# Attention with software-pipelined steps: a unit's first values half a step later, reciprocals of 64 columns, and the maxima's rows by six transfers

## The chip, the cores and the metric

The kernel runs on one core of one Trainium2 chip. The metric is the device time of one execution in microseconds (us), and lower is better. The median of three runs of the kernel before is 2694.99 us (2693.69 to 2695.18).

## The reference

Two sequences of 2048 tokens with 512 features go through one decoder layer with 16 heads of 32 features. All is in float32.

```python
x = x + attn(layernorm(x))      # Q, K, V = projections; scores = Q K^T / sqrt(32), rotary angles on Q and K
                                # softmax over all 2048 keys, times V, then W_o
x = x + xattn(layernorm(x))     # h = x ctx^T, gelu (tanh form), times ctx (77 rows)
x = x + ffn(layernorm(x))       # x sign(W)^T * scale + bias, clipped to +-100
```

## The kernel before

The work goes sequence by sequence (B = 2). `project_batch` makes Q, K and V for 16 chunks of 128 tokens. `Attention.run` then does the attention. It is this function that the change touches.

**Units and steps.** A unit is 256 queries (HQ) of one group g of four heads; there are NU = 32 units per sequence. A unit has STEPS = 8 steps of 256 keys each (two chunks c of 128). A step has two halves in `run`: the first does the scores of heads 0 and 1, the second those of heads 2 and 3. So a unit has 16 halves, and the document speaks of "step 1, second half" and so on.

**A half on TensorE.** The scores of two heads (`scores`, L603) go into banks `st`, while the maxima of the other two heads (`maxima`, L484) run on the other 32-row groups of the array. The maxima are those of a later unit, AHEAD = 11 steps in front. Each maxima matmul fills a bank of the pool `ps_s`, which has three. VectorE reduces it (L496) and so frees the bank. ScalarE takes the exponentials (L744), and POOL adds the two chunks of keys (L746). Then TensorE does the values of the step before (`weigh`, L621: four matmuls of 256 columns, chunk 0 in the first half by `first_half`, chunk 1 in the second by `second_half`) and the totals of the step before that (`total`, L635: four matmuls of 128 columns). A unit's totals begin two steps after the unit itself, so step 1 has none. At the end of step 0's second half the totals of the unit before are closed.

**The scores carry their maximum.** `st` isn't written anew in each step: the unit begins by writing minus the maximum of each query into it (`lower`, L584, a matmul of a row of ones with `mrow`), and each step adds the product of Q with a difference of keys (`key_steps`, `wrap_around`). The maximum is split into three bfloat16 parts (`split_maxima`, step 4), so `mrow` has three rows for each head, at partitions 32h, 32h + 1 and 32h + 2, in two column halves c.

**The rows' way.** In step 5's second half, `turn_maxima` transposes the parts on VectorE (L526), writes the square to DRAM (L528) and reads it back into `mrow` by small transfers (L532), all from SyncE's queue. The next unit's `lower` needs them.

**The division.** `divide` is a generator: ScalarE copies numerators and totals out of the accumulator bank (L649, the pool `ps_acc` has one), VectorE takes reciprocals (L655), POOL multiplies into the q tile (L658). `finish` takes one piece of it at a time, once per half. When the last unit of a block of queries is divided, `after_attention` for that block goes into `queue`.

**Background.** `after_attention` (W_o, layer norms, cross attention, feed forward) is a generator as well. `background(1)` runs one piece of it after every second half. In steps with odd t a light call also runs one after the first half, if the piece before it did not yield True (a piece that needs a wait or TensorE comes next); in the last ND = 4 units both halves call `background(1)`. Its tiles take banks from the same pool `ps_s`. Its outputs are written from SyncE's queue (L389).

**What sets the order.** In `run` the order on TensorE, VectorE, ScalarE and POOL is that of the program text (`manual_schedule`). SyncE's order is left to the framework's planner, which also makes the waits from the regions that each instruction reads and writes.

Of the kernel before, what the change touches and what calls it, by code (L numbers as in the profile page):

```python
# [16 lines left out]
P = 128  # L17
B, S, D = 2, 2048, 512
H, DK = 16, 32
# [17 lines left out]
def decoder_layer(  # L37
# [16 lines left out]
    nc = tc.nc  # L54
# [18 lines left out]
    def load_x(b, ch, pool=xpool):  # L73
        t = pool.tile([P, D], F32, tag="x", name=f"x_{b}_{ch}")
        nc.sync.dma_start(t, tokens(x[b], ch))
        return t
# [89 lines left out]
    def chunk_norm(ahead, b, ch, engine=nc.gpsimd):  # L166
        xc = ahead.pop(0)
        stats = stats_tile(1)
        chunk_stats(xc, stats[:, 0, 0:2])
        y, off = scale_and_shift(engine, stats)  # L170
        yield
        xn = work.tile([P, D], F32, tag="w", name="xn")
        nc.scalar.activation(xn, xc, AF.Identity, bias=off, scale=y)
        if ch + 2 < NCH:
            ahead.append(load_x(b, ch + 2))
        yield xn
# [255 lines left out]
    def background(n, light=False):  # L432
        while queue and n > 0 and not (light and heavy[0]):
            more = next(queue[0], queue)
            if more is queue:
                queue.pop(0)
                heavy[0] = False
            else:
                heavy[0] = more
                n -= 1  # L440
# [16 lines left out]
    class Attention:  # L457
# [57 lines left out]
        def turn_maxima(self, u):  # L515
            mrow = mrows[u % 2]
            if u == 0:
                pt = ps_s.tile([P, 2, P], BF16, tag="s", name="ptm")
                for c in range(2):
                    nc.tensor.transpose(  # L520
                        pt[:, c, :], first_mt[:, c].rearrange("p h d -> p (h d)"), ident_b
                    )
                nc.vector.tensor_copy(mrow, pt)
            else:
                square = small.tile([P, DK], BF16, tag="square", name="square")
                nc.vector.transpose(square, mts[u % 2].rearrange("p h n -> p (h n)"))  # L526
                rows = dram.tile([P, DK], BF16, tag="rows", name="rows")
                nc.sync.dma_start(rows, square)  # L528
                by_row = rows.rearrange("(a h n) i -> n a h i", a=4, h=4)
                for h in range(4):  # L530
                    for c in range(2):
                        nc.sync.dma_start(  # L532
                            mrow[h * DK : h * DK + 3, c].rearrange("n (a i) -> n a i", a=4),
                            by_row[3 * c : 3 * c + 3, :, h, :],
                        )
            self.mrow[u] = mrow.rearrange("p c q -> p (c q)")

# [107 lines left out]
        def divide(self, u):  # L645
            qb, g, hf = self.units[u]
            acc = self.acc.pop(u)
            num = work.tile([P, 2, HQ], F32, tag="w", name="num")
            nc.scalar.copy(num, acc)  # L649
            yield  # L650

            last = self.b == B - 1 and u == NU - 1
            for c in range(2):
                part = slice(c * P, (c + 1) * P)
                nc.vector.reciprocal(num[:, 1, part], num[:, 1, part])  # L655
                if not last:
                    yield
                (nc.vector if last else nc.gpsimd).tensor_mul(  # L658
                    self.q[qb][:, g, hf * HQ + c * P : hf * HQ + (c + 1) * P],
                    num[:, 0, part],  # L660
                    num[:, 1, part],
                )
            if g == ND - 1 and (hf == 1 or qb == NB - 1):
                first = hf * (CPB // 2) if qb == NB - 1 else 0
                late = self.b == B - 1 and qb == NB - 1
                size = 1 if late else (hf + 1) * (CPB // 2) - first
                for c in range(first, (hf + 1) * (CPB // 2), size):
                    (tail if late else queue).append(
                        after_attention(self.b, qb, self.q[qb], c, c + size)
                    )  # L670
# [14 lines left out]
        def run(self):  # L685
            prev = None
            sums_due = None
            ends = []

            def finish():  # L690
                while ends and next(ends[0], ends) is ends:
                    ends.pop(0)

            def first_half():
                if prev is not None:
                    self.weigh(prev, 0)
                if sums_due is not None:
                    self.total(sums_due, slice(0, P))

            def second_half():  # L700
                nonlocal sums_due
                if prev is not None:
                    self.weigh(prev, 1)
                if sums_due is not None:
                    self.total(sums_due, slice(P, HQ))
                sums_due = prev
                if prev is not None and prev[1] == STEPS - 1:
                    self.total(prev, slice(0, HQ))
                    ends.append(self.divide(prev[0]))
                    sums_due = None  # L710

            ordered = tc.manual_schedule(
                engines={
                    mybir.EngineType.PE,
                    mybir.EngineType.DVE,
                    mybir.EngineType.Activation,
                    mybir.EngineType.Pool,
                }
            )
            ordered.__enter__()  # L720
            attending.append(True)
            more = self.b + 1 < B
            for t in range(NU * STEPS):
                u, i = divmod(t, STEPS)
                if t == NU * STEPS - AHEAD:
                    free.append(True)
                if more and t == (NU - 1) * STEPS:
                    self.x_next = [load_x(self.b + 1, 0), load_x(self.b + 1, 1)]
                if more and t == NU * STEPS - STEPS // 2:
                    next_norm = chunk_norm(self.x_next, self.b + 1, 0)  # L730
                    next(next_norm)
                if more and t == NU * STEPS - 2:
                    xn = next(next_norm)
                pw = big.tile([P, 4, 2, HQ], F32, tag="s", name="pw")
                sm = sums.tile([P, 4, HQ], F32, tag="sm", name="sm")
                for heads, others in (((0, 1), (2, 3)), ((2, 3), (0, 1))):
                    if i == 0:
                        self.lower(u, heads)
                        self.wrap_around(self.units[u][1])
                    self.scores(u, i, heads, 0)  # L740
                    reduce = self.maxima(t + AHEAD, others)
                    self.scores(u, i, heads, 1)
                    for h in heads:
                        nc.scalar.activation(pw[:, h], self.st[h], AF.Exp, scale=SCALE)  # L744
                    hs = slice(heads[0], heads[1] + 1)
                    nc.gpsimd.tensor_add(sm[:, hs, :], pw[:, hs, 0, :], pw[:, hs, 1, :])  # L746
                    if reduce:
                        reduce()
                    if heads[0] == 0:
                        first_half()  # L750
                        finish()
                        if u >= NU - ND:
                            background(1)
                        elif t % 2 == 1:
                            background(1, light=True)
                    else:
                        finish()
                        second_half()
                        if prev is not None and prev[1] == STEPS - 1:
                            finish()  # L760
                        if (t + AHEAD) % STEPS == 0 and u + 1 < NU:
                            self.turn_maxima(u + 1)
                        if (t + AHEAD) % STEPS == STEPS - 1 and u + 1 < NU:
                            self.split_maxima(u + 1)
                        background(1)
                prev = (u, i, pw, sm)
            xnt = turn(xn) if more else None
            first_half()
            second_half()
            while ends:  # L770
                finish()
            attending.clear()
            free.clear()
            ordered.__exit__(None, None, None)
            return xnt
# [65 lines left out]
```

## Time and profile before

| | |
|---|---|
| median of 3 runs | 2694.99 us |
| the profiled execution's own time | 2694.35 us |
| its span | 2692.6 us |
| TensorE matmuls busy | 2666.4 us (99%) |
| VectorE, ScalarE, POOL busy | 64%, 49%, 65% |
| granted TensorE clock | 0.998 of full speed |

The page of the profile lists the busy time of each engine, the chain of work that ended last, and the costliest groups of instructions: line, engine, operation, tiles (out<-in), shapes and count, then busy us and mean ns of one, then the idle time before them and what ended it. The timeline lists instructions in order of time: start in us, duration in us, engine, line, operation, and in brackets the idle time before with what ended it. PE is TensorE, PEld its weight loads, DVE VectorE, ACT ScalarE, POOL GpSimd and SP (SPq) SyncE's queue. Consecutive instructions of one kind are merged into one row (x2, x8).

### The profile page before, as it was taken

What the parts mean: (1) busy time and instruction counts of PE and PEld (TensorE: products, weight loads), DVE (VectorE), ACT (ScalarE), POOL (GpSimd) and SP (SyncE); (2) the same over time, 40 slices, a digit from 0 to 9 for tenths busy, and PEclk for the clock granted to TensorE, in tenths of its full rate; (3) what the DMA queues carried; (4) which work ended last, traced back from release to release, by engine and by line L of the source; (5) the groups of instructions that cost most, each with busy time, mean ns of one, the idle gap of its engine ahead of it and who ended that gap; (6) DMA issues with size and microseconds to landing.
All of it is one profiled execution on the core that took longest, in us unless ns stands there. A gap on an engine that the chain in (4) does not pass through costs nothing.

```text
span 2692.6 us, 70762 instructions
## 1 busy us (share of the span) xinstructions
PE 2666.4 (99%) x30500; PEld 1475.8 (55%) x30500; DVE 1718.6 (64%) x2928; ACT 1323.3 (49%) x2394; POOL 1762.9 (65%) x1916
## 2 busy tenths in 40 slices
PE   8999999999999999999999999999999999999998
PEld 4445555555555555555554455555555555555555
DVE  3447777667766766676344477766767667766754
ACT  2214555455546554555422155555555455546553
POOL 3227777577857786777543287766787577857782
PEclk9999999999999999999999999999999999999999
DMA  3010000000000000000201000000000000000000
GB/s 126 24 32 2 3 2 2 2 2 18 18 2 2 10 26 2 2 10 25 76 24 40 5 2 3 2 3 2 2 26 10 2 2 18 18 2 2 18 18 17
DMA packets 36824, 40.65 MB, mean 15 GB/s; under 512 B 19206, under 2 KB 19718, under 8 KB 36512
## 3 DMA queue, kind: packets, MB, share of 16 engines
q1 hardware_dynamic: 36512, 36.14, 4.5%
q8 instruction: 239, 3.92, 0.6%
q14 instruction: 73, 0.60, 0.1%
HBM read 27.23 MB, written 8.90 MB: 13 GB/s over the span
## 4 chain that ended last, share of the span: by engine, by line
PE 98%; DVE 1%; DMA 0%; issue 0%; ACT 0%; SPq 0%; POOL 0%; POOLq 0%; ACTq 0%
PE st L603 24%; PE acc L621 22%; PE ps L484 18%; PE acc L635 8%; PE po L394 4%; PE pk L195 4%; PE pq L195 4%; PE pv L195 4%; PE pf L375 2%; PE st L584 2%; PE pt L357 1%; PE po L420 1%; PE ptqk L203 1%; PE ph L401 1%; PE pt L185 1%; DMA wk<-in_wk_t_dram 0%
## 5 line engine op out<-in xcount | busy, mean ns | idle before, releaser
L746 POOL TENSOR_TENSOR sm<-pw 128x512 f32<-128x512 f32 x1024 | 1297.9, 1274 | 567.4 <-ACT pw L744 563.1
L496 DVE TENSOR_REDUCE mx<-ps 128x1 f32<-128x512 f32 x2048 | 1309.1, 682 | 500.2 <-PE ps L484 498.3
L744 ACT ACTIVATE pw<-st 128x512 f32<-128x512 f32 x2048 | 1113.2, 596 | 942.0 <-PE ps L484 733.8
L484 PE MATMUL ps<-k,q 32*128 32x512 f32 x4096 | 1192.5, 639 | 1.5 <-DVE mx L496 1.5
L621 PE MATMUL acc<-pw,v 128*32 128x256 f32 x8192 | 655.0, 391 | 0.0
L635 PE MATMUL acc<-sm,ones 128*32 128x128 f32 x7680 | 388.3, 280 | 0.0
L621 PEld LDWEIGHTS acc<-pw,v 128*32 128x32 f32 x8192 | 161.9, 108 | 405.3 <-issue 386.9
L484 PEld LDWEIGHTS ps<-k,q 32*128 32x128 f32 x4096 | 356.8, 183 | 25.2 <-issue 13.7
L635 PEld LDWEIGHTS acc<-sm,ones 128*32 128x32 f32 x7680 | 247.2, 110 | 153.9
L603 PE MATMUL st<-q,dkk 32*128 32x256 f32 x2048 | 291.0, 400 | 0.0
L603 PE MATMUL st<-q,dkv 32*128 32x256 f32 x2048 | 289.9, 400 | 0.0
L603 PE MATMUL st<-q,dkq 32*128 32x256 f32 x2048 | 289.9, 400 | 0.0
L603 PEld LDWEIGHTS st<-q,dkk 32*128 32x128 f32 x2048 | 175.0, 184 | 89.5 <-issue 51.4
L603 PEld LDWEIGHTS st<-q,dkq 32*128 32x128 f32 x2048 | 172.7, 184 | 80.0 <-issue 54.2
L603 PEld LDWEIGHTS st<-q,dkv 32*128 32x128 f32 x2048 | 174.7, 184 | 58.9 <-issue 26.4
L231 POOL TENSOR_TENSOR r<-r 128x512 f32<-128x512 f32 x64 | 81.2, 1268 | 162.4 <-DVE r L230 150.6
L655 DVE RECIPROCAL num<-num 128x128 f32<-128x128 f32 x128 | 120.6, 943 | 54.2 <-ACT num L649 54.2
L603 PE MATMUL st<-q,wrap 32*128 32x256 f32 x1024 | 144.9, 400 | 0.0
L603 PE MATMUL st<-q,k 32*128 32x256 f32 x1024 | 133.2, 375 | 0.0
L149 DVE BATCH_NORM_STATS2 st<-x 128x6 f32<-128x512 f32 x96 | 65.4, 686 | 93.6 <-DMA x<-in_x_dram 93.2
L195 PE MATMUL pk<-wk,xnt 128*128 128x512 f32 x256 | 118.1, 605 | 3.4 <-DMA wk<-in_wk_t_dram 2.0
L394 PE MATMUL po<-wo,q 128*128 128x512 f32 x256 | 117.4, 603 | 0.0
(114 smaller groups left out, 1953.8 us busy)
## 6 DMA issues: line engine op xcount, KB each, us to landing
x<-in_x_dram SPq DMA_DIRECT2D x64, 256.0 KB
out_dram<-x SPq DMA_DIRECT2D x32, 256.0 KB
mrow<-rows SPq DMA_DIRECT2D x496, 0.8 KB
wk<-in_wk_t_dram SPq DMA_DIRECT2D x2, 1024.0 KB
wq<-in_wq_t_dram SPq DMA_DIRECT2D x2, 1024.0 KB
wv<-in_wv_t_dram SPq DMA_DIRECT2D x2, 1024.0 KB
wo<-in_wo_t_dram SPq DMA_DIRECT2D x1, 1024.0 KB
wf<-in_wf_t_dram SPq DMA_DIRECT2D x1, 1024.0 KB
```

The lines of the kernel that those rows point to most:

```text
L149: nc.vector.bn_stats(st, xc)
L195: nc.tensor.matmul(dst, xnt[:, i, :], w[:, i, :], start=(i == 0), stop=(i == ND - 1))
L231: nc.gpsimd.tensor_add(r[:, 0, a], r[:, 0, a], r[:, 1, a])
L394: nc.tensor.matmul(ps, ot[:, i, cols], wo[:, i, :], start=(i == 0), stop=(i == ND - 1))
L484: nc.tensor.matmul(ps, self.q[qb][self.rows[h], g, q0 : q0 + P], self.k[kb][self.rows[h], g, :], start=True, stop=True,)
L496: nc.vector.tensor_reduce(mx[:, qc, h, kb : kb + 1], ps, AX.X, ALU.max)
L603: nc.tensor.matmul(self.st[h][:, c, :], keys[r, g, kc * P : (kc + 1) * P], self.q[qb][r, g, hf * HQ : (hf + 1) * HQ], start=False, stop=Tr ...
L621: nc.tensor.matmul(acc[self.rows[h], 0, :], self.v[self.chunk(i, c)][:, d0 : d0 + DK], pw[:, h, c, :], start=(i == 0 and c == 0), stop=(i ...
L635: nc.tensor.matmul(acc[self.rows[h], 1, part], ones, sm[:, h, part], start=False, stop=(i == STEPS - 1), skip_group_check=True,)
L655: nc.vector.reciprocal(num[:, 1, part], num[:, 1, part])
L744: nc.scalar.activation(pw[:, h], self.st[h], AF.Exp, scale=SCALE)
L746: nc.gpsimd.tensor_add(sm[:, hs, :], pw[:, hs, 0, :], pw[:, hs, 1, :])
```

## The change

It has three parts.

1. In step 1 of each unit, `first_half` (the unit's first value matmuls, chunk 0) no longer runs in the first half but in the second, just ahead of `second_half`. The piece of the division and the light background call of that first half are left out there; the division's pieces so begin in the second half of step 1.
2. The reciprocals are taken in four operations of 64 columns, each a piece of its own, where there were two of 128 columns. The very last unit keeps two of 128.
3. `mrow` is read back by six transfers where there were eight: one for each of the three parts and two column halves, with one row of each of the four heads (partitions n, n + 32, n + 64, n + 96), where there was one for each head and column half with the three parts of that head.

```diff
-                by_row = rows.rearrange("(a h n) i -> n a h i", a=4, h=4)
-                for h in range(4):
+                by_row = rows.rearrange("(a h n) i -> n h a i", a=4, h=4)
+                for n in range(3):
                     for c in range(2):
                         nc.sync.dma_start(
-                            mrow[h * DK : h * DK + 3, c].rearrange("n (a i) -> n a i", a=4),
-                            by_row[3 * c : 3 * c + 3, :, h, :],
+                            mrow[n::DK, c].rearrange("h (a i) -> h a i", a=4),
+                            by_row[3 * c + n],
                         )
...
                 part = slice(c * P, (c + 1) * P)
-                nc.vector.reciprocal(num[:, 1, part], num[:, 1, part])
-                if not last:
-                    yield
+                size = P if last else P // 2
+                for k in range(c * P, (c + 1) * P, size):
+                    nc.vector.reciprocal(num[:, 1, k : k + size], num[:, 1, k : k + size])
+                    if not last:
+                        yield
...
                     if heads[0] == 0:
-                        first_half()
-                        finish()
+                        if i != 1:
+                            first_half()
+                            finish()
                         if u >= NU - ND:
                             background(1)
-                        elif t % 2 == 1:
+                        elif t % 2 == 1 and i != 1:
                             background(1, light=True)
                     else:
                         finish()
+                        if i == 1:
+                            first_half()
                         second_half()
```

## The prediction

> **What bounds the kernel now.** I read the page first: busy shares, then the chain that ended last, then the groups.
>
> ```profile
> span 2692.6 us, 70762 instructions
> PE 2666.4 (99%) x30500; PEld 1475.8 (55%) x30500; DVE 1718.6 (64%) x2928; ACT 1323.3 (49%) x2394; POOL 1762.9 (65%) x1916
> ...
> PE 98%; DVE 1%; DMA 0%; issue 0%; ACT 0%; SPq 0%; POOL 0%; POOLq 0%; ACTq 0%
> ...
> L496 DVE TENSOR_REDUCE mx<-ps 128x1 f32<-128x512 f32 x2048 | 1309.1, 682 | 500.2 <-PE ps L484 498.3
> ...
> L655 DVE RECIPROCAL num<-num 128x128 f32<-128x128 f32 x128 | 120.6, 943 | 54.2 <-ACT num L649 54.2
> ```
>
> TensorE is the bound from end to end, so the change is worth what it does to the moments at which TensorE can start its next group. Busy shares hide short stalls (matmul ends are modelled). So I went on to the timeline of TensorE's weight loads, in a unit with no other work (batch 0, unit 3, steps 1 and 2):
>
> ```profile
> 311.29 0.19 PEld L603 LDWEIGHTS st<-q,dkk 32*128 32x128 f32 x2 [0.41 <-ACT pw L744]
> ...
> 312.36 0.16 PEld L621 LDWEIGHTS acc<-pw,v 128*32 128x32 f32 x8 [0.34 <-ACT num L649]
> 312.93 0.19 PEld L603 LDWEIGHTS st<-q,dkk 32*128 32x128 f32 x2 [0.41 <-issue]
> ...
> 314.26 0.16 PEld L621 LDWEIGHTS acc<-pw,v 128*32 128x32 f32 x8 [0.60 <-issue]
> 314.83 0.19 PEld L603 LDWEIGHTS st<-q,dkq 32*128 32x128 f32 x2 [0.41 <-issue]
> ...
> 316.26 0.16 PEld L621 LDWEIGHTS acc<-pw,v 128*32 128x32 f32 x8 [0.70 <-issue]
> ...
> 317.05 0.19 PEld L603 LDWEIGHTS st<-q,dkq 32*128 32x128 f32 x2 [0.20 <-issue]
> ...
> 318.26 0.16 PEld L621 LDWEIGHTS acc<-pw,v 128*32 128x32 f32 x8 [0.48 <-issue]
> ...
> 319.05 0.19 PEld L603 LDWEIGHTS st<-q,dkv 32*128 32x128 f32 x2 [0.20 <-ACT pw L744]
> ```
>
> The first score load of a half is its start, the first L621 load its values. Four halves (step 1, step 2) take 1.64, 1.90, 2.22 and 2.00 us, 7.76 together. From start to values they take 1.07, 1.33, 1.43 and 1.21; later halves alternate 1.07 and 1.11. So 0.26 + 0.36 + 0.14 = 0.76 us per unit is lost here. VectorE's timeline in the same place says why:
>
> ```profile
> 312.47 1.29 DVE L496 TENSOR_REDUCE mx<-ps 128x1 f32<-128x512 f32 x2 [1.11 <-PE ps L484]
> 313.67 0.94 DVE L655 RECIPROCAL num<-num 128x128 f32<-128x128 f32 x1
> 314.53 1.22 DVE L496 TENSOR_REDUCE mx<-ps 128x1 f32<-128x512 f32 x2
> 315.67 0.94 DVE L655 RECIPROCAL num<-num 128x128 f32<-128x128 f32 x1
> 316.52 1.22 DVE L496 TENSOR_REDUCE mx<-ps 128x1 f32<-128x512 f32 x2
> ```
>
> Two maxima per half share three banks (the pool of three), so a half's second maxima wait for the first reduction of the half before. That reduction starts 1.18 us after its half (312.47 - 311.29), lasts 0.68, and its bank is loaded again 1.92 after the start (at 313.21). Values follow that load by 1.05 (314.26). Step 1 has no totals, so its first half is short and the second waits: 0.26. Then a reciprocal holds the next reduction from 314.11 (312.93 + 1.18) to 314.53, and the second one the next but one: 0.36 and 0.14.
>
> Last, SyncE's queue where the rows come late (batch 0, unit 12, for unit 13), and the first operation that waits:
>
> ```profile
> 636.63 0.34 SPq L528 DMA_DIRECT2D rows<-square  x1
> 641.68 0.36 SPq L389 DMA_DIRECT2D out_dram<-x  x1
> 642.15 2.75 SPq L532 DMA_DIRECT2D mrow<-rows  x8
> ```
> ```profile
> 644.05 0.09 PEld L584 LDWEIGHTS <-ones_b 32*128 32x128 bf16 x1 [0.20 <-DMA mrow<-rows]
> 644.48 0.09 PEld L584 LDWEIGHTS <-ones_b 32*128 32x128 bf16 x1 [0.33 <-DMA mrow<-rows]
> ```
>
> Each head has its own two transfers now. Head 0's load goes at 644.05, head 1's 0.43 later, when the fourth transfer (issued 643.13 to 643.40) has landed: 1.07 after its issue ended.
>
> **First values half a step later.** In step 1 the first value group (four matmuls of 256 columns) leaves the first half and stands in front of the second one. Its cost: a half with totals takes 0.79 from values to the next start, one without 0.57, so four matmuls of 128 columns are 0.22 and four of 256 are 0.43. What it leaves is no gain: the second half starts earlier (about 0.9 instead of 1.64), but its second maxima still wait for the bank at 1.92, so values still start at 2.97, now two groups of them. The next half starts at 2.97 + 0.43 + 0.57 = 3.97 instead of 3.54. The cover was real: the group lay inside VectorE's time. The trace shows this case once per batch. At its start three score groups stand without values between them, 215.89 to 220.06, 4.17 us; without the banks it would be some 0.97 + 0.97 + 1.07 = 3.0 (a score group 0.86, as below, and 0.11 for the unit's rows: its halves reach values after 1.18). The ScalarE copy of num, which the group also waits for, is no bound: in this unit it asks for nothing beyond the 1.07 of any free half. Pool buffers are let go by the second group as before.
>
> The row has a value group follow a score group after some 0.2 us (1.07 against the 0.86 that two 256-column score blocks stream). The Trainium skill, "TensorEngine Tiling (Array Packing)", Key Properties, says that changing the tiling mode drains TensorE; one drain each way would go, some 0.2 to 0.4 us per unit, by the rule a gain of 12 to 25 us in all. By the rows that time falls into the wait for the bank, and the gain is nothing.
>
> **Reciprocals.** Two of 943 ns become four. The 128x512 and 128x128 tensor operations of VectorE take 688 and 293 ns, so a fixed 160; a reciprocal's column is then 6.1 ns, and 64 columns take 0.55. Start to start the long one takes 0.86 (313.67 to 314.53); a short one 0.86 - 64 x 6.1 ns = 0.47. Bounds: 0.43 (half) and 0.55 (nothing overlapped); I take 0.47, by the pitch. Between a half's reductions VectorE stands idle 0.57 us in regular halves, so one fits, and the stalls of 0.36 and 0.14 go. Clean unit: 3.97 + 1.86 + 1.90 = 7.73 against 7.76.
>
> The Trainium skill, "VectorE: DVE Perf Modes", section on the TRN2 errata, speaks against it: each VectorE operation on SBUF pays a fixed cost, so at least 512 elements are advised. By that two more operations cost 0.3 us per unit, 19 us of VectorE; in the sum that is nothing while the gap covers it.
>
> The gap is not always free. The divide now ends in step 3's second half instead of step 2's first; three reciprocals sit where other work of VectorE comes. POOL's two products (461 ns each) move one step and one and a half later in its queue; only POOL's sums stand behind them, which have over a step, and POOL is 65% busy. I followed the background queue piece by piece through the old and the new calls. Step 1 loses its light call, but a piece that TensorE must follow waits for a second half anyway, so nearly all stay where they were; the four outputs per batch issued in step 5 stay too. Where it matters:
> - Units 9, 11, 17, 19, 25, 27: TensorE's background piece in step 1's second half already hid the second and third stall, so 0.43 is a pure loss. A bn_stats and bn_aggr pair (0.82) in step 2's second half now follows a reciprocal: the next reduction is 0.6 late, the half after next 0.4 longer. +0.83 each.
> - Units 10, 18, 26, 29: only one stall to win, +0.05. Unit 30 has background work in step 1's first half: -0.5. Unit 0 +0.1, unit 31 (no maxima) -0.3.
> - Units 8, 16, 24: a bn_stats leaves the place where it stalled a half (1.42 instead of 1.11): -0.3. The other 16: -0.05 (7.73 to 7.76 and its rounding).
>
> Per batch 6 x 0.83 + 4 x 0.05 - 0.5 + 0.1 - 0.3 - 3 x 0.3 - 16 x 0.05 = +2.8 us; two batches +5.6. With bounds of 0.1 per ordinary unit (44 of them) and the 0.4 absent or doubled: 0 to +12.
>
> **Six transfers.** 496 issues become 372, each about 0.32 apart, so the queue is free 0.65 sooner. But each transfer now carries one row of all four heads, so heads 0 and 1, which start the unit, need all six where they needed the first four. Ready is now the first issue + 2.32 (3 x 0.325 + 0.27 + 1.07), then + 2.97. A usual unit starts 4.5 or more after the first issue: hidden. Eight units (13, 14, 21, 22 of each batch, behind an output transfer that waits for POOL) start 1.9 after it. Their stalls, 3.7 us in all now, become 8 x 1.05 less one luckier unit, 8.0: +4.3. The load has four more waits of TensorE's sequencer, 0.125 apart; it reaches them 0.77 ahead of the load, so five end 0.14 ahead: nothing, 0.1 per unit if that is too late. Transfers behind on SyncE (x loads, outputs) go sooner, with nobody waiting. Bounds: -3.7 (all late waits gone) to +18 (serial, below).
>
> **Sum.** The profiled execution took 2694.35, 1.75 more than its span and 0.64 less than the median of 2694.99. 2694.35 + 5.6 + 4.3 = 2704.3; against the median 2704.9. I say 2704.5.
>
> **The rivals.**
> - *The transfers run one after another.* Each writes partitions 32 apart; if the planner takes these spans as overlapping, each waits for the one before in its column half: first issue + 4.40. Compared with every unit's start this gives 22.0 us of stalls against 3.7: 2695 + 5.6 + 18.2 = 2719. Against it: a ScalarE copy into columns 0 to 127 of a q tile (1257.61 to 1258.20) lets TensorE read columns 256 on at 1257.73 unhindered, so interleaved columns are told apart; partitions with a step do not occur.
> - *The rows stay hidden.* If the planner puts the rows ahead of the outputs in SyncE's queue, the eight late units are no longer late: 2695 + 5.6 - 3.7 = 2697, no measurable change.
> - *Faster: the bank comes back sooner.* If in step 1 the second maxima got their bank at 1.49 or sooner instead of 1.92, the moved group would cost nothing: 62 x 0.43 = 27 us less, 2678. For it: the score group in front is earlier. Against: the reduction can't start before 1.18 and lasts 0.68, and the start of the batch.
>
> **How the numbers follow.** Likeliest case 0.54 (its own range 2699 to 2710), serial transfers 0.18 (2713 to 2722), rows hidden 0.16 (2692 to 2702), faster 0.09, and 0.03 for something slower than all. About 0.2% (5.4 us) is what a measurement of this kernel tells from no change: below 2689.6 is faster, above 2700.4 slower. Faster 0.09; same 0.18 (most of the third case, a tenth of the first); slower 0.73. The range 2695 to 2720 leaves out the faster case, some of the third and the top of the second.
>
> **What would show it.** In a clean unit: no L621 load in step 1's first half, sixteen together some 2.97 after its start, the next half at 3.97, then 1.86 and 1.90; reciprocals near 0.55 inside the idle of VectorE; in unit 9 a half with 1.6 to its values in step 3; in units 13, 14, 21, 22 a first L584 load about 1.05 late, and 372 row issues. Wrong would make it: values of step 1 well before 2.97, reciprocals that don't shrink with their columns, or row issues a microsecond apart.

## The result, and the profile after

The changed kernel takes 2735.27 us (median of 4 runs, 2732.25 to 2737.34) against 2694.69 us for the kernel before in the same comparison: a ratio of 1.015, with a 95% interval of 1.0136 to 1.0164. It is slower by 40.6 us, where about 10 were predicted. The profiled execution took 2737.34 us, its span is 2735.6 us, 43.0 more than before.

The page after: span, TensorE's busy share, the chain that ended last by engine, and the two groups of VectorE that were shown of before.

```profile
span 2735.6 us, 70524 instructions
...
PE 2683.7 (98%) x30500; PEld 1487.4 (54%) x30500; DVE 1739.4 (64%) x3054; ACT 1320.7 (48%) x2394; POOL 1761.1 (64%) x1916
...
PE 96%; DMA 1%; SPq 1%; DVE 1%; issue 0%; ACT 0%; POOL 0%; POOLq 0%; ACTq 0%
...
L496 DVE TENSOR_REDUCE mx<-ps 128x1 f32<-128x512 f32 x2048 | 1315.2, 685 | 508.6 <-PE ps L484 474.9
...
L658 DVE RECIPROCAL num<-num 128x64 f32<-128x64 f32 (+1 forms) x254 | 137.9, 545 | 53.1 <-ACT num L649 53.1
```

SyncE's queue and the DMA each have a per cent of the chain now, where they had none, and TensorE is busy for 17 us more with the same 30500 matmuls. Both are followed below. First the two parts that the page hardly shows: TensorE's weight loads in a unit with no other work (batch 0, unit 4, steps 1 and 2).

```profile
343.28 0.19 PEld L603 LDWEIGHTS st<-q,dkk 32*128 32x128 f32 x2 [0.41 <-ACT pw L747]
...
345.20 0.18 PEld L484 LDWEIGHTS ps<-k,q 32*128 32x128 f32 x1 [0.75 <-DVE mx L496]
...
346.25 0.59 PEld L621 LDWEIGHTS acc<-pw,v 128*32 128x32 f32 x16 [0.74 <-ACT pw L747]
347.25 0.19 PEld L603 LDWEIGHTS st<-q,dkq 32*128 32x128 f32 x2 [0.41 <-ACT pw L747]
...
348.32 0.16 PEld L621 LDWEIGHTS acc<-pw,v 128*32 128x32 f32 x8 [0.34 <-issue]
...
349.11 0.19 PEld L603 LDWEIGHTS st<-q,dkq 32*128 32x128 f32 x2 [0.20 <-issue]
...
350.22 0.16 PEld L621 LDWEIGHTS acc<-pw,v 128*32 128x32 f32 x8 [0.38 <-issue]
...
351.01 0.19 PEld L603 LDWEIGHTS st<-q,dkv 32*128 32x128 f32 x2 [0.20 <-ACT pw L747]
```

Step 1 starts at 343.28. It has no values in its first half. The second maxima wait for their bank until 345.20 (1.92 after the start), the sixteen value loads go together at 346.25 (2.97), and the next half starts at 347.25 (3.97). Then come halves of 1.86 and 1.90. VectorE in the same place:

```profile
346.97 0.54 DVE L658 RECIPROCAL num<-num 128x64 f32<-128x64 f32 x1
348.43 1.29 DVE L496 TENSOR_REDUCE mx<-ps 128x1 f32<-128x512 f32 x2 [0.91 <-PE ps L484]
349.63 0.54 DVE L658 RECIPROCAL num<-num 128x64 f32<-128x64 f32 x1
350.29 1.29 DVE L496 TENSOR_REDUCE mx<-ps 128x1 f32<-128x512 f32 x2
```

A short reciprocal lies between two pairs of reductions and delays none.

Now the rows. The chain of waits, cut to the moment when unit 13 of batch 0 starts (start in us, duration in us, what):

```profile
by line: SPq L532 39.8%; DMA mrow<-rows 31.0%; issue 10.3%; PE st L584 9.7%; PE st L603 7.4%; PE ps L484 3.5%
...
645.62 0.38 SPq L532
646.00 0.04 issue
646.04 0.51 SPq L532
646.55 0.04 issue
646.60 0.50 SPq L532
...
648.23 1.86 DMA mrow<-rows
650.09 0.40 issue
650.49 0.58 PE st L584
```

This stretch is bound by the issuing of six transfers, 0.50 us each, and the landing of the last. SyncE's queue and the first load and matmul of unit 13:

```profile
645.01 0.34 SPq L389 DMA_DIRECT2D out_dram<-x  x1
645.47 3.26 SPq L532 DMA_DIRECT2D mrow<-rows  x6
```
```profile
650.45 0.13 PEld L584 LDWEIGHTS <-ones_b 32*128 32x128 bf16 x2 [3.25 <-issue]
```
```profile
650.49 0.61 PE L584 MATMUL st<-mrow,ones_b 32*128 32x512 bf16 x2 [3.04 <-DMA mrow<-rows]
```

TensorE's work for unit 12 ended at 647.4; unit 13 begins at 650.45, 4.98 us after the first issue and 1.72 after the end of the last. The table of engines by stretch, for the time after that wait (the columns are the stretch and its length, busy us and count of each engine, then the granted TensorE clock, DMA share and GB/s):

```profile
640.00:647.00 7.00, 7.00 (x108) 4.00 (x105) 4.80 (x8) 4.80 (x9) 6.92 (x6) 1.00 0.11 39
...
650.40:654.00 3.60, 3.52 (x30) 2.08 (x30) 1.29 (x2) 1.09 (x2) 0.00 (x0) 0.50 0.14 49
...
657.00:660.00 3.00, 3.00 (x32) 1.94 (x24) 0.72 (x2) 1.18 (x3) 1.29 (x1) 1.00 0.00 0
```

After the wait TensorE runs at half clock (0.50) for several microseconds. The trace of before has no such stretch inside the attention.

**Where the 43.0 us of span went**, half by half against the trace of before, both batches: steps 1 to 7 without the last half of step 7 (the first two parts of the change) +5.8; the last half of step 7, at whose end a unit waits for the next one's rows, +27.1, of which the waits ahead of the eight units 13, 14, 21 and 22 of both batches are 21.7 (2.3 to 3.0 each); step 0 +8.6, which is the kernel before's 3.7 of stalls gone and some 12.3 lost to the half clock (27.3 us at half clock follow seven of the eight waits, worth at most 13.7); elsewhere +1.6.

### The profile page after: what moved, and what is told of

The parts are those of the page before. It is cut to its first block, busy times and chain, and to the rows that moved or that the text cites. A ratio compares the mean times of both kernels' runs of the same rounds, so it can differ in the third digit from the quotient of the medians.

```text
span 2735.6 us, 70524 instructions
## 1 busy us (share of the span) xinstructions
PE 2683.7 (98%) x30500; PEld 1487.4 (54%) x30500; DVE 1739.4 (64%) x3054; ACT 1320.7 (48%) x2394; POOL 1761.1 (64%) x1916
## 4 chain that ended last, share of the span: by engine, by line
PE 96%; DMA 1%; SPq 1%; DVE 1%; issue 0%; ACT 0%; POOL 0%; POOLq 0%; ACTq 0%
PE st L603 23%; PE acc L621 21%; PE ps L484 18%; PE acc L635 8%; PE po L394 4%; PE pk L195 4%; PE pq L195 4%; PE pv L195 4%; PE pf L375 2%; PE st L584 2%; SPq L532 1%; PE pt L357 1%; PE po L420 1%; PE ptqk L203 1%; PE ph L401 1%; DMA mrow<-rows 1%
## 5 line engine op out<-in xcount | busy, mean ns | idle before, releaser
L484 PE MATMUL ps<-k,q 32*128 32x512 f32 x4096 | 1212.2, 642 | 1.5 <-DVE mx L496 1.5
L621 PE MATMUL acc<-pw,v 128*32 128x256 f32 x8192 | 644.6, 392 | 0.0
L484 PEld LDWEIGHTS ps<-k,q 32*128 32x128 f32 x4096 | 346.6, 183 | 72.2 <-DVE mx L496 54.3
L621 PEld LDWEIGHTS acc<-pw,v 128*32 128x32 f32 x8192 | 168.7, 108 | 385.2 <-issue 329.5
L603 PEld LDWEIGHTS st<-q,dkk 32*128 32x128 f32 x2048 | 164.0, 184 | 67.8 <-ACT pw L747 31.6
L658 DVE RECIPROCAL num<-num 128x64 f32<-128x64 f32 (+1 forms) x254 | 137.9, 545 | 53.1 <-ACT num L649 53.1
L339 DVE TENSOR_TENSOR x<-po,x 128x512 f32<-128x512 f32 x64 | 44.2, 691 | 117.8 <-PE po L394 91.7
```

The costliest lines, as they stand in the source:

```text
L484: nc.tensor.matmul(ps, self.q[qb][self.rows[h], g, q0 : q0 + P], self.k[kb][self.rows[h], g, :], start=True, stop=True,)
L603: nc.tensor.matmul(self.st[h][:, c, :], keys[r, g, kc * P : (kc + 1) * P], self.q[qb][r, g, hf * HQ : (hf + 1) * HQ], start=False, stop=Tr ...
L621: nc.tensor.matmul(acc[self.rows[h], 0, :], self.v[self.chunk(i, c)][:, d0 : d0 + DK], pw[:, h, c, :], start=(i == 0 and c == 0), stop=(i ...
L658: nc.vector.reciprocal(num[:, 1, k : k + size], num[:, 1, k : k + size])
```

## The experiments

The theory after the comparison is that the first two parts do what was predicted, and that the new transfers cost the rest: each takes SyncE 0.50 us to issue instead of 0.27. The rivals were that the parts disturb each other, and then, for the long issue, several properties of the new transfers.

**The rows alone and the rest alone.** `rows_only` has the third part of the diff, `without_rows` the first two.

> Part 3 alone: the kernel before with six transfers. Theory A (the transfers are the mis-sized term: an issue of four partitions takes 0.50 us instead of 0.27, so the rows are ready 4.3 us or more after the first issue, and TensorE's clock drops after the longest waits): 2728 to 2736 us, stalls in units 13, 14, 21 and 22 of each batch of 2.3 to 3 us, half-speed stretches behind some of them, steps 1 to 3 unchanged (7.76 us in a clean unit). Theory B (the six transfers only hurt because the other two parts moved the work around them): 2695 to 2705 us.

> Parts 1 and 2 together with the eight transfers of before. Theory A: the 5.6 us of the prediction's first term, 2698 to 2703 us, with 2.97 us to the values of step 1 and 3.97 to the next half, and stalls of 0.4 us in the eight late units as before. Theory B: most of the loss stays, 2720 us or more.

Measured: rows_only 2726.33 us (ratio 1.0123, 1.0108 to 1.0138), without_rows 2699.15 us (1.002, 1.001 to 1.0029), the kernel before 2693.75 us beside them. Rows_only is 1.7 us below the range of theory A and far from theory B. In it steps 1 to 7 without the last half are unchanged (each step within 0.06 us in all), the last halves are 26.2 us longer and step 0 5.8. TensorE's waits for DMA in rows_only (us in total, times, longest):

```profile
PE st L584 <- DMA mrow<-rows: 26.2, 14, 2.8
```

In the kernel before that row reads 0.3 us. So the parts add up: 32.6 + 5.4 = 38.0 of 40.6 us. The remaining 2.6 is less than the width of the intervals (about 8 us each for the whole change and rows_only); the traces differ in the number of half-clock stretches (seven after late rows in the whole change, five here).

**The first two parts apart.** `recip_only` has the reciprocals alone. `values_only` moves the first values alone:

```diff
                     if heads[0] == 0:
-                        first_half()
+                        if i != 1:
+                            first_half()
                         finish()
...
                         finish()
+                        if i == 1:
+                            first_half()
                         second_half()
```

> Part 2 alone: four reciprocals of 64 columns, everything else as before. By the same recurrence of bank and VectorE that gave the prediction: the stalls of 0.36 and 0.14 go and nothing is paid for them, except where a bn_stats follows the fourth reciprocal; 2676 to 2682 us, clean unit's four halves 1.64, 1.90, 1.86, 1.90. Rival: more VectorE operations delay the reductions elsewhere: 2690 us or more.

> Part 1 alone: the first values in step 1's second half; division, light background calls and the two long reciprocals as before. By the recurrence the moved group costs 0.43 us a unit and the bank's wait moves on to hide the second and third stall in part: 2697 to 2702 us. Rival (the saved change between score and value groups is a gain): 2690 us or less.

Measured: recip_only 2678.37 us (0.9942, 0.9925 to 0.9958), values_only 2696.19 us (1.001, 1.0001 to 1.0019), beside 2693.75 us. The time of values_only is 0.8 us below its expected range, and its interval only just excludes no change; either way it is no gain. The short reciprocals are the gain of the change, 15.4 us. VectorE in recip_only, batch 0, unit 3, steps 1 and 2, the place that the prediction showed of before:

```profile
311.04 0.54 DVE L657 RECIPROCAL num<-num 128x64 f32<-128x64 f32 x1
311.50 1.26 DVE L496 TENSOR_REDUCE mx<-ps 128x1 f32<-128x512 f32 x2
312.68 0.54 DVE L657 RECIPROCAL num<-num 128x64 f32<-128x64 f32 x1
313.37 1.29 DVE L496 TENSOR_REDUCE mx<-ps 128x1 f32<-128x512 f32 x2 [0.15 <-PE ps L484]
```

From a reciprocal's start to the reduction behind it are 0.46 us, against 0.86 of the long one. The halves of these two steps take 1.64, 1.90, 1.86 and 1.90: the stalls of 0.36 and 0.14 are gone and the first value group costs nothing where it stood. With the values moved as well, step 1 pays the 0.43 and has no stall of its own to win back. In values_only step 2's halves take 1.86 and 1.93 with the long reciprocals still there: moving the values cures the same stalls by itself, and pays for it. So the two parts are two cures of one ill, and only the second is free.

**Is it the number of partitions that makes an issue long?** `four_rows` keeps the eight transfers of before and pads each to four neighbouring partitions, 16 pieces as in the change (the fourth is not used).

```diff
-                by_head = mts[u % 2][:, :, 0:6].rearrange("p h (c n) -> p c h n", n=3)
+                by_head = mts[u % 2].rearrange("p h (c n) -> p c h n", n=4)
...
-                            mrow[h * DK : h * DK + 3, c].rearrange("n (a i) -> n a i", a=4),
-                            by_row[3 * c : 3 * c + 3, :, h, :],
+                            mrow[h * DK : h * DK + 4, c].rearrange("n (a i) -> n a i", a=4),
+                            by_row[4 * c : 4 * c + 4, :, h, :],
```

`three_heads` keeps the step of 32 partitions and takes three heads instead of four, 12 pieces as before.

```diff
-                            mrow[n::DK, c].rearrange("h (a i) -> h a i", a=4),
-                            by_row[3 * c + n],
+                            mrow[n : n + 65 : DK, c].rearrange("h (a i) -> h a i", a=4),
+                            by_row[3 * c + n, :3],
```

(This diff is against the changed transfers; the rest of the kernel is before's.)

> The kernel before, still eight transfers, one for each head and column half, but each carries four adjacent partitions (the three parts and a row of zeros), so 16 pieces of 64 bytes instead of 12. Theory P (the four partitions make the issue long): an issue of 0.50 us; heads 0 and 1 need four of them, ready 3.2 to 3.7 us after the first issue, stalls of 1.3 to 1.8 us in the eight late units, 2702 to 2710 us. Theory S (the step of 32 between partitions makes it long): issues of 0.27 us as before, 2692 to 2696 us.

> Six transfers with partitions 32 apart as in the change, on the kernel before, but for three heads only: 12 pieces of 64 bytes each. The rows of head 3 are left out, so that head's scores keep no maximum (they are as long to compute). Theory P (four partitions): issues of 0.27 us, ready first issue + 2.97, the prediction's own 4.3 us: 2696 to 2700 us. Theory S (step of 32): issues of 0.50 us, as long as in the change, 2720 us or more.

Measured: four_rows 2695.34 us (1.0006, 0.9996 to 1.0015), three_heads 2763.31 us (1.0262, 1.0246 to 1.0277), beside 2693.97 us. The issues of the row transfers (count, then min/median/max in ns, first and last start in us), in the kernel before, after, in four_rows and in three_heads:

```profile
L532 SPq DMA_DIRECT2D mrow<-rows x496: 232/268/662, 241.0 to 2611.7; - x166
```
```profile
L532 SPq DMA_DIRECT2D mrow<-rows x372: 499/500/687, 240.4 to 2653.6; - x186
```
```profile
L532 SPq DMA_DIRECT2D mrow<-rows x496: 241/292/540, 240.9 to 2611.3; - x166
```
```profile
L532 SPq DMA_DIRECT2D mrow<-rows x372: 683/688/816, 239.3 to 2678.9; - x186
```

Four neighbouring partitions cost 24 ns more than three; three partitions with a step cost 420 ns more. The number is not the cause. That three with a step take longer than four with the same step was expected by no theory, and stays open.

**The step in DRAM or the step in partitions?** The change made both sides of a transfer strided. `dram_step` keeps the changed source and writes neighbouring partitions; `sbuf_step` reads neighbouring rows of DRAM, in eight transfers, and writes partitions 32 apart.

```diff
-                            mrow[n::DK, c].rearrange("h (a i) -> h a i", a=4),
+                            mrow[n * DK : n * DK + 4, c].rearrange("h (a i) -> h a i", a=4),
```

(dram_step, against the changed transfers, the rest as before; below sbuf_step, against before, with the padding of four_rows)

```diff
-                            mrow[h * DK : h * DK + 3, c].rearrange("n (a i) -> n a i", a=4),
-                            by_row[3 * c : 3 * c + 3, :, h, :],
+                            mrow[h::DK, c].rearrange("n (a i) -> n a i", a=4),
+                            by_row[4 * c : 4 * c + 4, :, h, :],
```

> The change's six transfers alone, with the same source (one row of four heads, 512 bytes apart in DRAM, 16 pieces), but written to four adjacent partitions instead of four partitions 32 apart. It changes the computation: the rows of the maxima land on the wrong partitions, so only its times are read. If the step of 32 between partitions makes an issue long, an issue takes 0.27 to 0.30 us as in the kernel before and the time is 2688 to 2698 us. If the step in DRAM makes it long, an issue takes 0.50 us and the time is 2715 to 2732 us.

> Eight transfers as in the kernel before, each from neighbouring rows of one head in DRAM (16 pieces), but written to four partitions 32 apart. It changes the computation: the rows of the maxima land for the wrong heads, so only its times are read. If the step between partitions makes an issue long, an issue takes about 0.50 us, eight of them 4.0 us instead of 2.7, and the late units lose 3 us or more each: 2725 to 2765 us. If the step in DRAM makes it long, an issue takes 0.27 to 0.30 us and the time is 2692 to 2705 us.

Measured: dram_step 2696.51 us (1.0003, 0.9993 to 1.0013), sbuf_step 2772.74 us (1.0286, 1.0266 to 1.0307), beside 2695.64 us. Their issues:

```profile
L532 SPq DMA_DIRECT2D mrow<-rows x372: 241/292/619, 240.4 to 2611.9; - x186
```
```profile
L532 SPq DMA_DIRECT2D mrow<-rows x496: 499/500/703, 239.0 to 2689.5; - x166
```

This settles it: the step between the partitions written makes the issue long, and the step in DRAM does not. Eight such issues take 4.37 us from the first to the end of the last, and the late units of sbuf_step wait 3.7 to 4.1 us. Its time is 8 us above the range that was expected for it: 31.6 of the 62.4 us by which its last halves grow lie in usual units, whose rows are late too. The time of dram_step says nothing of the dependencies, since there head 0's partitions are written by two of the six transfers only.

**What does it cost that the first heads need all the rows?** `heads_reversed` issues before's eight transfers from head 3 to head 0, so that the head that starts the unit has its rows last.

```diff
-                for h in range(4):
+                for h in reversed(range(4)):
```

> The kernel before with its eight transfers issued from head 3 to head 0, so that heads 0 and 1 wait for the last one: ready first issue + 3.6 to 3.7 us, stalls of about 1.7 us in the eight late units, 10 us more than before. If TensorE's clock drops only after a stall of some 2.5 us, no half-speed stretch is seen and the time is 2702 to 2706 us; if any wait of that kind drops it, 2712 us or more.

Measured: 2715.13 us (1.0077, 1.0062 to 1.0092), beside 2693.97 us. SyncE's queue and the wait at unit 13 of batch 0:

```profile
641.46 2.53 SPq L532 DMA_DIRECT2D mrow<-rows  x8
...
645.15 0.22 PEld L584 LDWEIGHTS <-ones_b 32*128 32x128 bf16 x2 [1.97 <-DMA mrow<-rows]
```

The load goes 3.69 us after the first issue. By the prediction's rule for when the rows are ready it is 7 x 0.325 + 0.27 + 1.07 = 3.62. So the rule holds where the issues are short. The eight late units wait 1.64 to 2.05 us, and the last halves grow by 14.3 us in all, which is the whole of the 14.2 that this profiled execution's span is longer. Its own time is the lowest of its four runs (2708.68 to 2718.61); where the longer ones lose the rest isn't shown. One stretch at half clock follows a wait of 1.69 us here, and none follows the seven other waits, so neither side of the expectation (none, or any wait of that kind) holds as it stands; the last section takes this up.

**Are the rows late only because of what stands ahead of them?** `after_outputs_pool` is the whole change, and `recip_outputs_pool` is recip_only, both with the outputs of line 389 issued from POOL's queue while a batch is attended to.

```diff
-            nc.sync.dma_start(tokens(out[b], blk * CPB + first + c), xs[c])
+            (nc.sync if alone or free else nc.gpsimd).dma_start(
+                tokens(out[b], blk * CPB + first + c), xs[c]
+            )
```

> The whole change, and the outputs that are sent while a batch is attended to (line 389) are issued from POOL's own queue, so that on SyncE's queue no row transfer stands behind an output that waits for POOL. The computation is whole. Theory A (the rows of units 13, 14, 21 and 22 are late because their six issues of 0.50 us each begin only when the output ahead of them has been let go, and each such wait of 2.3 to 3.0 us can bring a stretch at half clock): the rows' first issue moves some 3 us or more forward in these eight units, their waits at line 584 go to below 0.3 us and no stretch at half clock follows them. That takes away about 20 us of waits and 10 us of half clock: 2701 to 2708 us. Theory B (six transfers of four partitions are late for a reason of their own, whatever stands ahead on the queue): the waits stay, 2730 us or more. A price that may show: POOL issues the outputs itself; if an issue holds POOL's sums back, stalls at another place, some 0.5 us each in eight places, 4 us.

> The kernel before with the four short reciprocals alone (which measured 2678.4 us) and the outputs of line 389 issued from POOL's own queue while a batch is attended to. The computation is whole. In the kernel before, the eight late units lose 3.7 us in all at line 584. Theory A (those rows are late only because they stand behind an output on SyncE's queue): these 3.7 us go, 2673 to 2676 us. Rival: POOL pays for issuing the outputs and holds its sums back, 2678 to 2684 us.

Measured: after_outputs_pool 2707.51 us (1.0043, 1.0028 to 1.0058), recip_outputs_pool 2679.95 us (0.9942, 0.9926 to 0.9959), beside 2695.64 us. In after_outputs_pool the late units' rows go out early, with the same long issues (unit 13 of batch 0):

```profile
640.25 3.26 SPq L534 DMA_DIRECT2D mrow<-rows  x6
```
```profile
646.18 0.09 PEld L586 LDWEIGHTS <-ones_b 32*128 32x128 bf16 x2 [0.17 <-issue]
```

The waits there vanish, as does every half-clock stretch after a wait. What is left of the waits for rows:

```profile
PE st L586 <- DMA mrow<-rows: 5.3, 6, 1.4
```

These are usual units, whose rows stood behind no output: rows that are ready 4.5 us and more after the first issue are too late for some of them as well. So the long issue needs the output ahead to do its full harm, and does some without it. The price of POOL's issuing is real: 26 issues of 0.61 us each (mean 0.63) stand in POOL's sums, and in both kernels steps 4 to 6 grow by 4.5 and 5.9 us against the same kernel with the outputs on SyncE. In recip_outputs_pool that eats the 3.7 us won in step 0, and the ratio is that of recip_only; the rival was right there.

**Does it matter where the pieces of the division lie?** `recip_first_halves` has the four short reciprocals, and takes pieces of the division in first halves alone.

```diff
                     else:
-                        finish()
                         second_half()
```

> Part 2 alone, and the division's pieces taken in first halves only (steps 1, 2, 3, 4 and 5), so that no reciprocal stands in front of a bn_stats, which come in second halves. If the 0.4 us behind these pairs is what step 3 lost in units 9, 11, 17, 19, 25 and 27, 4 to 5 us less than part 2 alone: 2671 to 2676 us. Rival: the block's background starts 1.5 steps later and its pieces stall elsewhere: 2678 us or more.

Measured: 2686.13 us (0.9972, 0.996 to 0.9983), beside 2693.97 us. Unit 3's halves are as in recip_only (1.64, 1.90, 1.86, 1.90), but the division ends later, and pieces of the background move behind it: in unit 9 step 3 now has a half of 5.62 us where recip_only has one of 2.40. Most of such a difference is work moved from one unit to another (in the same traces unit 8 is 3.95 us shorter and unit 9 2.95 longer); where the net loss arises isn't shown. It wins half of what recip_only does, and the rival of its expectation was right. The fastest of all twelve are recip_only and recip_outputs_pool, both 0.9942 of the kernel before.

## Why the prediction was wrong

Its sign was right, and its size was not: 2704.5 us was predicted, with 2695 to 2720 as the range.

- **First values half a step later: right.** Values 2.97 after step 1's start, the next half at 3.97, the bank again at 1.92. The moved group is no gain. The rule on drained tiling modes, from the Trainium skill, "TensorEngine Tiling (Array Packing)", Key Properties, would have made it a gain of 12 to 25 us by the prediction's estimate; the trace after and values_only (+2.4 us) show none, for the second maxima wait for their bank until 1.92 all the same. Whether TensorE drains there, no run shows.
- **Short reciprocals: right.** 545 ns where 0.55 us was worked out, 0.46 from start to start where 0.47 was taken. The stalls of 0.36 and 0.14 went. The fixed cost that the Trainium skill, "VectorE: DVE Perf Modes", section on the TRN2 errata, warns of is there (2 x 545 - 943 = 147 ns for each pair), and the gap hides it: recip_only is 15 us faster.
- **The collisions with the background: right.** Units 9, 11, 17, 19, 25 and 27 became 0.84 longer (0.83 predicted), with 1.61 to the values in step 3 of unit 9. Both parts together: +5.4 us by time and +5.8 by the trace, where the sum had +5.6. That it agrees to 0.2 is in part luck: unit 31 of each batch became 0.9 shorter where 0.3 was predicted and unit 0 0.2 shorter where it was to lose 0.1, while in the second batch unit 29 became 0.86 longer where 0.05 was predicted and unit 30 won 0.03 instead of 0.5.
- **Six transfers: wrong, and this is the step that failed.** The term was "each about 0.32 apart", and from it "the first issue + 2.97". The issues measure 0.50 us and stand 0.55 apart: six take 3.26 us instead of 1.90. The first load goes 1.25 to 1.73 us after the last issue's end, where 1.07 was taken. In the eight late units the first load so comes 4.53 to 4.98 us after the first issue. The price of a transfer that writes partitions with a step was taken from rows of transfers that write neighbouring ones, at the one place where the trace of before had no row; the prediction itself said that partitions with a step do not occur there. It used this against the rival of serial transfers, and not as an unknown of its own with a bound. The last sentence ("row issues a microsecond apart") saw the possibility, and the range did not take it in.
- **"A usual unit starts 4.5 or more after the first issue: hidden": wrong by the same term.** The 4.5 was also read too high: in the trace of before seven of the 54 usual units start only 3.54 to 4.47 us after their first issue. With 2.97 a margin of 0.57 us or more was left all the same; with 4.5 to 5 it is gone, and six usual units have last halves 0.6 to 1.2 us longer, 5.2 us in all.
- **Not foreseen: the clock.** Some 12 of the 43.0 us of span are lost after the waits, not in them. The eight waits themselves were put at 8.0 in all; they became some 22.
- **The rivals.** The transfers do not run one after another: in the late units the issues follow at 0.55 us and none waits for a landing. The time lies beyond that rival's 2719 all the same; that its readiness (first issue + 4.40) and its 22.0 us of stalls come near the measured 4.53 to 4.98 and 26.9 is luck, since the cause it gave does not occur. The rows did not stay hidden, and the bank did not come back sooner.

With the measured readiness the prediction's own method comes close. A late unit starts some 1.9 us after its first issue if its rows are there. 4.53 to 4.98 less 1.9 is 2.6 to 3.1 of wait for each, eight make 21 to 25, less the 3.7 that were there, and the clock on top.

## What to carry to other kernels

The cost of issuing a transfer is a property of its shape, and here the step between the partitions written doubled it, while fewer transfers had been the count to watch; a shape that the trace doesn't show is an unknown with a bound on each side, even when there are fewer of them and their bytes in all stay the same (8 x 12 and 6 x 16 pieces of 64 bytes). A late transfer of a few microseconds on the bound engine can be paid for twice, since TensorE's clock was halved after seven of the eight such waits here. And when two edits cure the same stall, each should be priced with the other in place: the short reciprocals alone were worth 15 us, and the moved values turned that into a loss of 5.

## What the runs showed of the hardware

**What an issue costs.** On SyncE's queue a transfer of 64-byte pieces (12 for three partitions, 16 for four) takes 0.27 us to issue (medians) for three neighbouring partitions, 0.29 for four, 0.29 for four from strided DRAM, 0.50 for four partitions 32 apart, and 0.69 for three partitions 32 apart.

**When the clock falls.** Between 220 and 2650 us the stretches at half clock last 3.41 or 6.83 us, and within one execution they all start a multiple of 3.41 us apart. If each of nine traces (before, after, rows_only, four_rows, three_heads, heads_reversed, dram_step, sbuf_step, after_outputs_pool) is cut, from 220 to 2650 us, into windows of that length in phase with its first stretch, and TensorE's idle time is summed in each window that runs at full clock, the windows with 0.9 us or more sort like this:

```
idle in the window, us     windows    followed by half clock
0.9 to 1.6                      33                         0
1.6 to 1.8                       4                         1
1.8 to 2.5                      17                        17
2.5 to 3.41                     17                        17
```

So what counted was the idle time in one window, and the border lies near half of it. This fits one wait of 2.55 us in the changed kernel (batch 0, unit 14) that left the clock alone: its two windows have 0.85 and 1.73 us of idle. It also fits heads_reversed, where four waits of 1.77 to 2.05 us, each cut by a border, left the clock alone and one of 1.69, whole in its window, did not. Four traces have one more such stretch, at the change of sequence (at 1564.3 us in the changed kernel), with only 0.76 us of idle in front; there TensorE ran the first unit's maxima alone, on 32 rows of the array each. The other five traces run this stage at full clock; what decides it isn't shown. The Trainium skill, "TensorE: Matmul & The Clock Gate", Part 1, has a free-running window of 3413 ns, and these traces agree with that; its rule of no idle gaps above some 3 us, in the section on why this matters for kernels, is too mild for them: a wait of 1.69 us sufficed once, and every window with 1.84 us or more of idle did.
